# Folding the values of layer 1: one run of matmuls for each pair, two engines to empty its banks, and a bias on VectorE

## Chip, cores and metric

The kernel runs on one core of a Trainium2 chip. The metric is the device time of one execution in microseconds. Every input and output is float32. TensorE multiplies, VectorE (DVE) and ScalarE (ACT) do elementwise work and are the ones that read the matmuls' result banks (PSUM), GpSimd (POOL) does elementwise work, SyncE (SP) issues most transfers.

## What is computed

Two cross-attention layers in sequence, on 4 batches of 1024 tokens with 1024 channels and a context of 64 tokens a batch (the reference, cut; the norm over the context, the masks and the head shapes are left out):

```python
# layer 0: 32 query heads, 8 key heads
out = softmax(q(x) @ k(ctx).T * scale + mask0) @ v(ctx)     # per head
r   = out @ Wo + bo + x
x1  = (r - mean(r)) * rsqrt(var(r) + 1e-6) * gamma + beta
# layer 1: 16 heads
a   = layer_norm(ctx)
out = softmax((x1 @ Wq.T) @ (a @ Wk.T).T * scale) @ (a @ Wv.T)
y   = x1 + tanh(gate) * (out @ Wo.T)
```

## The kernel before

The work is in stages. Stage 1 computes layer 0's queries and attention and leaves its head outputs turned in DRAM (oTd). **Stage 2**, the one that the change is in, multiplies these by Wo, adds bo and x, normalizes, and stores x1. Stage 3 is layer 1.

Layer 1 is folded: since the context has only 64 tokens, keys are multiplied into Wq (`folded_queries`, stage 1) and values into Wo (`folded_values`, in stage 2), once for each batch, so that stage 3 has one 1024x1024 product for the scores and one for the outputs. Both folded matrices go to DRAM (ad and bd) and are read back in stage 3.

**Pairs.** Stage 2 goes over 16 pairs of 128-token tiles (`for pair in range(1, NPAIR)`, L1098; pair 0 is begun before the loop). A pair's product with Wo is Winograd's form of Strassen's algorithm, `products` at L435: seven products of half size, each four matmuls of 128x128x512, with accumulating banks. In the order of the list at L470, called P1 to P7 here:

- P1 = A11 B11 and P2 = S2 T2 and P4 = S1 T1 and P5 = S4 B22 go into one bank X, each added onto what the bank holds; after each, VectorE adds the bank's state to a half row of the result (L455), and the next product of X can only start once that read is done.
- P3 = S3 T3 and P6 = A22 N4 likewise in a bank V; P7 = A12 B21 alone in a bank W.

The sums S1, S2, S4 and S3 of the left side are made by VectorE (`left_out`, L429 to L432) for the next pair, at the place of P6 of the pair before (`tail`). Four banks of 512 columns rotate (pool ps_wx); two tiles of two banks each (pool ps_big, function `two`) serve the fold.

**Rows.** r_0, r_1, ... are tiles of 128 rows x 1024 channels, two for each pair (r_2, r_3 for pair 1). `load_outputs` (L947), called one pair ahead, loads the pair's heads o and its two rows of x into r, and, for all pairs but the first, adds bo to them on GpSimd (L958). The pool of r has six buffers, so a load for pair p + 2 waits until pair p - 1's row has been stored. L455 then adds the products on top. `close_rows` (L1051) normalizes a finished pair on VectorE, a row at a time: two BNStats (L292), an aggregate (L297), L298, a square root on ACT (L299), L306, L302, L309, and a store by SyncE (L1053). These steps are given to the next pair's `project` (L481) as a list `fill`, and a share of it is taken after each of its seven products.

**The fold of the values.** For pair 1 to 8, `folded_values(vT, wch, pair - 1)` is put onto `fill`: one chunk of 128 channels, as two calls of `keys` (one for two batches each). Each call has two pieces (n = 0, 1); a piece is two matmuls, one on the lower and one on the upper 64 rows of TensorE (e = 0, 1), into the two banks of one tile of `two()`. ACT copies both banks, times tanh(gate), to a tile st (L929), and SyncE stores st to bd in two transfers (L933). A chunk thus has four pieces, and two tiles of banks for them. The profile shows each float32 matmul as two records.

The order of instructions on each engine isn't that of the text alone: a scheduler moves them by its own priorities and by the waits between them, except those under `keep_in_program_order`. In the program as built, TensorE's rows of a pair of stage 2 stand as P1, one matmul of P3, P2, the rest of P3, P4, one matmul of P6, P5, the rest of P6, P7, and before the change a chunk of the fold stands behind P7 (in pair 1 in three parts). Each engine works through its own queue in order, and waits at its head.

Of the kernel before, what the change touches and what calls it, by code (L numbers as in the profile page):

```python
# [10 lines left out]
AF = mybir.ActivationFunctionType  # L11
ALU = mybir.AluOpType
# [16 lines left out]
NPAIR = NSUB // 2  # L29
# [42 lines left out]
def tile_two_cross_attentions(  # L72
# [25 lines left out]
    nc = tc.nc  # L98

    def sub_ap(t):  # L100
        return slice(t * P, (t + 1) * P)
# [31 lines left out]
    def open_pool(stack, name, bufs, side="left"):  # L133
        return stack.enter_context(tc.tile_pool(name=name, bufs=bufs, side=side, reuse_waits="tile"))
# [68 lines left out]
    def right_weight(w, tag, name, turned=False):  # L203
        r, loads = right_loads(w, tag, name, turned)
        run(loads)
        return r, right_sums(r)

    def run(steps):
        for s in steps:
            s()  # L210
# [74 lines left out]
    def normalize_steps(t, eps, name, late=False, scaled=None):  # L285

        st = small.tile([P, 2, 6], F32, tag="st", name=f"st_{name}")
        mv = small.tile([P, 2], F32, tag="mv", name=f"mv_{name}")
        rstd = small.tile([P, 1], F32, tag="rstd", name=f"rstd_{name}")

        def stats(i):
            r = nc.vector.bn_stats(st[:, i, :], t[:, i * 512 : (i + 1) * 512])  # L292
            if late:
                tc.keep_in_program_order(r)

        def deviation():
            nc.vector.bn_aggr(mv, st.rearrange("p a b -> p (a b)"))  # L297
            nc.vector.tensor_scalar(rstd, mv[:, 1:2], eps, None, ALU.add)  # L298
            nc.scalar.activation(rstd, rstd, AF.Sqrt)  # L299

        def scale():
            nc.vector.reciprocal(rstd, rstd)  # L302
            if not scaled:
                nc.vector.tensor_scalar(t, t, mv[:, 0:1], rstd, ALU.subtract, ALU.mult)
                return
            nc.vector.scalar_tensor_tensor(t, t, mv[:, 0:1], scaled[0], ALU.subtract, ALU.mult)  # L306

        def shift():
            nc.vector.scalar_tensor_tensor(t, t, rstd, scaled[1], ALU.mult, ALU.add)  # L309

        return [lambda: stats(0), lambda: stats(1), deviation, scale] + ([shift] if scaled else [])
# [73 lines left out]
    tanh_gate = const.tile([P, 1], F32, tag="tanh", name="tanh_gate")  # L385
# [4 lines left out]
    def two():  # L390
        b = big()
        return [b[:, 0:512], b[:, 512:1024]]
# [31 lines left out]
    def left_out(o, pool, name):  # L424

        a11, a21 = o[:, 0:HK, 0:P], o[:, 0:HK, P : 2 * P]
        a12, a22 = o[:, HK:KC, 0:P], o[:, HK:KC, P : 2 * P]
        s = {n: pool.tile([P, HK, P], F32, tag=n, name=f"{n}_{name}") for n in ("S1", "S2", "S4")}
        nc.vector.tensor_tensor(s["S1"], a21, a22, ALU.add)  # L429
        nc.vector.tensor_tensor(s["S2"], s["S1"], a11, ALU.subtract)  # L430
        nc.vector.tensor_tensor(a21, a11, a21, ALU.subtract)
        nc.vector.tensor_tensor(s["S4"], a12, s["S2"], ALU.subtract)  # L432
        return {"A11": a11, "A12": a12, "A22": a22, "S3": a21, **s}
# [443 lines left out]
    def chunk(w, k, name):  # L877
        t = wpool.tile([P, H], F32, tag="wb", name=f"{name}_{k}")
        nc.sync.dma_start(out=t, in_=w[sub_ap(k), :])
        return t  # L880
# [34 lines left out]
    def folded_values(vT, wch, c):  # L915


        def keys(bp):
            st = wpool.tile([P, 2, H], F32, tag="wb", name=f"b_{c}_{bp}")
            for n in range(2):  # L920
                banks = two()
                for e in range(2):
                    q = slice(e * S, (e + 1) * S)
                    nc.tensor.matmul(  # L924
                        banks[e], vT[q, c, sub_ap(bp)], wch[q, n * 512 : (n + 1) * 512],
                        start=True, stop=True,
                    )
                for e in range(2):
                    nc.scalar.activation(  # L929
                        st[:, e, n * 512 : (n + 1) * 512], banks[e], AF.Copy, scale=tanh_gate[:, 0:1]  # L930
                    )
            for b2 in range(2):
                nc.sync.dma_start(  # L933
                    out=bd[bp * 2 + b2, sub_ap(c), :].rearrange("(e s) o -> s e o", e=2),
                    in_=st[b2 * S : (b2 + 1) * S],
                )

        return [lambda bp=bp: keys(bp) for bp in range(2)]

    def load_o(pair, pool, tag="o2"):  # L940
        o = pool.tile([P, KC, 2 * P], F32, tag=tag, name=f"o2_{pair}")
        load = nc.sync.dma_start(out=o, in_=oTd[pair])
        if pair < 2:
            tc.keep_in_program_order(load)
        return o

    def load_outputs(pair):  # L947
        o = load_o(pair, o2pool) if pair > 1 else second if pair else load_o(0, early)
        r = []
        for u in range(2):  # L950
            t = pair * 2 + u
            ru = (rpool.tile([P, H], F32, tag="r", name=f"r_{t}") if pair
                  else early.tile([P, H], F32, tag="r", name=f"r_{t}", bufs=2))
            load = nc.sync.dma_start(out=ru, in_=x[sub_ap(t), :])
            if not pair:
                tc.keep_in_program_order(load)
            if pair:
                nc.gpsimd.tensor_tensor(ru, ru, bo_sb, ALU.add)  # L958
            r.append(ru)
        return o, r  # L960

# [62 lines left out]
    for t in range(last):  # L1024
        n = 28 - AHEAD if t // SUB == NBLK - 2 else 28
        mix(t, (t % SUB + 1) * n // SUB - t % SUB * n // SUB)
    go_on(FOLD_AHEAD)
    n = 4 * KC - FOLD_AHEAD + FIRST
# [22 lines left out]
    def close_rows(pair, r):  # L1051
        def last(u):
            nc.sync.dma_start(out=x1[pair][sub_ap(u), :], in_=r[u])  # L1053

        steps = []
        for u in range(2):
            steps += normalize_steps(
                r[u], EPS0, f"0_{pair * 2 + u}", True, (gamma0_sb, beta0_sb)
            ) + [lambda u=u: last(u)]
        return steps  # L1060
# [3 lines left out]
    def load_x1(pair):  # L1064
        xq = xqpool.tile([P, 2 * NQ, QW], F32, tag="xq", name=f"xq1_{pair}")
        load_quarters(xq, x1[pair])
        return xq

    def turn_x1(pair, xq, pool=None, tag="xT"):

        xT = (pool or xTpool).tile([P, KC, 2 * P], F32, tag=tag, name=f"xT_{pair}")

        def half(h):
            turn_quarters(xq, xT[:, h * HK : (h + 1) * HK, :], (h * HK, (h + 1) * HK))

        def blocks():
            lefts[pair] = left_out(xT, lpool if pool else lxpool, f"x_{pair}")

        return [lambda: half(0), lambda: half(1), blocks]
# [10 lines left out]
    open_stage()  # L1090
    _, ahead_r = load_outputs(1)
    run(first)

    fill = [
        lambda u=u: nc.vector.tensor_tensor(first_rows[u], first_rows[u], bo_sb, ALU.add) for u in range(2)
    ]
    fill += close_rows(0, first_rows)
    for pair in range(1, NPAIR):  # L1098
        r, a = ahead_r, ahead_a
        if pair + 1 < NPAIR:  # L1100
            ahead_o, ahead_r = load_outputs(pair + 1)
        if pair <= KC:
            ahead_w = chunk(wo1, pair, "wo1") if pair < KC else None
            fill += folded_values(vT, wch, pair - 1)
            wch = ahead_w
        if pair == KC + 2:
            w_a, w_a_sums = right_weight(ad[0], "wb", "a0", True)
        if pair in (NPAIR - 3, NPAIR - 2):
            fill += w_a_sums[0:2] if pair == NPAIR - 3 else w_a_sums[2:4]
        if pair == 3:  # L1110
            early_cm.close()
            xTpool = open_pool(last_cm, "x1T", 1)
            lxpool = open_pool(last_cm, "leftx", 1)
            xqpool = open_pool(last_cm, "x1q", 1)
        if pair == NPAIR - 4:
            xq = load_x1(1)
        if pair == NPAIR - 3:
            fill += turn_x1(1, xq)

        def tail():  # L1120
            nonlocal ahead_a
            if pair + 1 < NPAIR:
                ahead_a = left_out(ahead_o, lpool, f"0_{pair + 1}")
            else:
                turned[2]()

        project(a, w_o, r, fill, tail=tail)
        fill = close_rows(pair, r)
        if pair == NPAIR - 2:
            xq = load_x1(0)  # L1130
            turned = turn_x1(0, xq, o2pool, "o2")
            fill = turned[:2] + fill
# [78 lines left out]
    for pair in range(NPAIR):  # L1211
        r = []
        for u in range(2):
            ru = rpool.tile([P, H], F32, tag="r", name=f"r1_{pair}_{u}")
            nc.sync.dma_start(out=ru, in_=x1[pair][sub_ap(u), :])
            r.append(ru)
        fill = []
# [79 lines left out]
```

## Time and profile before

| | |
|---|---|
| median of 3 runs | 1915.06 us (1913.88 to 1915.12) |
| profiled execution | 1915.11 us, span 1913.3 us, granted TensorE clock 0.995 |
| TensorE busy | 1868.9 us (98%) |
| VectorE / ACT / GpSimd busy | 1292.1 (68%) / 427.9 (22%) / 179.1 us (9%) |
| stage 2 | from about 716 to 1130 us |
| L929, ACT's copies of the fold | 64 of 128x512, 687 ns each |
| L958, GpSimd's bias | 30 of 128x1024, 2354 ns each (median) |
| L1095, VectorE's bias for pair 0 | 2 of 128x1024, 1226 ns each |

Times in the profile are in us from the start of the span. A line of the timeline is: start, length, engine, source line, operation, output<-input, count, and in brackets how long the engine had been idle before and whose end released it. SPq, PEq and the like are the engines' sequencers, which issue transfers and wait for semaphores.

### The profile page before, as it was taken

What the parts mean: (1) busy time and instruction counts of PE and PEld (TensorE: products, weight loads), DVE (VectorE), ACT (ScalarE), POOL (GpSimd) and SP (SyncE); (2) the same over time, 40 slices, a digit from 0 to 9 for tenths busy, and PEclk for the clock granted to TensorE, in tenths of its full rate; (3) what the DMA queues carried; (4) which work ended last, traced back from release to release, by engine and by line L of the source; (5) the groups of instructions that cost most, each with busy time, mean ns of one, the idle gap of its engine ahead of it and who ended that gap; (6) DMA issues with size and microseconds to landing.
All of it is one profiled execution on the core that took longest, in us unless ns stands there. A gap on an engine that the chain in (4) does not pass through costs nothing.

```text
span 1913.3 us, 17522 instructions
## 1 busy us (share of the span) xinstructions
PE 1868.9 (98%) x6096; PEld 880.0 (46%) x6096; DVE 1292.1 (68%) x1582; ACT 427.9 (22%) x1396; POOL 179.1 (9%) x212
## 2 busy tenths in 40 slices
PE   8999999999998899999999999999999999999999
PEld 7744444444455653343344444444444444444444
DVE  3425589789878985575568778557665766576653
ACT  1101575666536751212100001000000000000000
POOL 0016011111100103121113100000000000000000
PEclk9999999999999899999999999999999999999999
DMA  8996599899878966567473363466656565657421
GB/s 276 184 222 192 158 253 247 253 252 261 252 186 275 302 234 207 188 207 238 164 218 138 121 141 90 110 165 158 150 143 165 150 158 143 165 142 165 121 88 44
DMA packets 220745, 350.54 MB, mean 183 GB/s; under 512 B 26992, under 2 KB 146160, under 8 KB 215664
## 3 DMA queue, kind: packets, MB, share of 16 engines
q1 hardware_dynamic: 152896, 242.44, 45.8%
q0 software_dynamic: 15216, 60.83, 10.5%
q10 hardware_dynamic: 52544, 46.14, 8.8%
q8 instruction: 48, 0.79, 0.2%
q14 instruction: 41, 0.34, 0.1%
HBM read 207.53 MB, written 141.82 MB: 183 GB/s over the span
## 4 chain that ended last, share of the span: by engine, by line
PE 82%; DVE 8%; DMA 5%; issue 2%; ACT 2%; POOL 0%; SPq 0%; DVEq 0%; POOLq 0%; ACTq 0%
PE wx L446 59%; PE wx L576 14%; PE big L680 2%; DMA pq<-p 2%; PE big L924 1%; PE wx L379 1%; PE big L379 1%; DVE s L684 1%; PE big L759 1%; DMA p<-s 1%; DMA q<-qTd 1%; DVE s L715 1%; DVE mx L691 1%; DVE sm L711 1%; DMA o<-oTd 1%
## 5 line engine op out<-in xcount | busy, mean ns | idle before, releaser
L455 DVE TENSOR_TENSOR r<-wx,r 128x512 f32<-128x512 f32 x224 | 153.5, 686 | 230.1 <-PE wx L446 215.3
L698 ACT ACTIVATE s<-s,mx 128x64 f32<-128x64 f32 x488 | 162.8, 335 | 74.9 <-DVE mx L691 70.7
L502 ACT ACTIVATE s<-s 128x1024 f32<-128x1024 f32 x32 | 33.7, 1057 | 651.7 <-DVE s L501 651.7
L459 DVE TENSOR_TENSOR s<-wx,key_bias 128x512 f32<-128x512 f32 x64 | 44.1, 690 | 136.7 <-PE wx L446 136.7
L446 PE MATMUL wx<-wo_B,S 128*128 128x512 f32 x256 | 117.1, 600 | 1.5 <-DVE r L455 1.5
L576 PE MATMUL wx<-xT,wq_S 128*128 128x512 f32 x256 | 116.5, 598 | 0.8 <-ACT z L587 0.8
L446 PE MATMUL wx<-b_B,pT 128*128 128x512 f32 x256 | 115.8, 593 | 0.6 <-ACT pT L414 0.6
L446 PE MATMUL wx<-b_B,S_p 128*128 128x512 f32 x256 | 116.0, 596 | 0.0
L446 PE MATMUL wx<-a_B,xT 128*128 128x512 f32 x256 | 115.4, 592 | 0.0
L446 PE MATMUL wx<-a_B,S_x 128*128 128x512 f32 x256 | 115.3, 593 | 0.1
L576 PE MATMUL wx<-xB,wq_A 128*128 128x512 f32 x256 | 115.1, 597 | 0.0
L446 PE MATMUL wx<-wo_B,o 128*128 128x512 f32 x256 | 114.8, 596 | 0.0
L958 POOL TENSOR_TENSOR r<-r,bo 128x1024 f32<-128x1024 f32 x30 | 78.5, 2625 | 313.8 <-DMA r<-in_x_dram 159.4
L684 DVE TENSOR_TENSOR s<-big,m 128x1024 f32<-128x1024 f32 x64 | 77.4, 1215 | 28.4 <-PE big L680 26.8
L680 PEld LDWEIGHTS big<-kv,q 64*128 64x128 f32 x1024 | 71.1, 195 | 48.3 <-issue 39.9
L698 ACT ACTIVATION_READ_ACCUMULATOR s<-s,mx 128x1 f32 x488 | 91.4, 187 | 0.0
L680 PE MATMUL big<-kv,q 64*128 64x128 f32 x1024 | 82.6, 292 | 2.6 <-DMA q<-qTd 2.6
L419 DVE STREAM_TRANSPOSE pT<-pq 128x1024 f32<-128x1024 f32 x66 | 78.0, 1219 | 3.3 <-DMA pq<-p 3.3
L446 PEld LDWEIGHTS wx<-wo_B,S 128*128 128x128 f32 x256 | 47.1, 190 | 67.7 <-issue 51.2
L715 DVE TENSOR_TENSOR s<-s,sm 128x1024 f32<-128x1024 f32 x64 | 77.0, 1216 | 0.9
L446 PEld LDWEIGHTS wx<-wo_B,o 128*128 128x128 f32 x256 | 47.8, 190 | 63.5 <-issue 62.3
L446 PEld LDWEIGHTS wx<-a_B,S_x 128*128 128x128 f32 x256 | 48.5, 190 | 62.0 <-issue 58.4
(162 smaller groups left out, 2903.5 us busy)
## 6 DMA issues: line engine op xcount, KB each, us to landing
p<-s POOLq DMA_DIRECT2D x19, 1024.0 KB, 8.1
pq<-p POOLq DMA_DIRECT2D x76, 256.0 KB, 6.0
xq<-in_x_dram SPq DMA_DIRECT2D x64, 256.0 KB, 10.2
q<-qTd SPq DMA_DIRECT2D x32, 512.0 KB, 7.4
oTd<-oT ACTq DMA_DIRECT2D x32, 512.0 KB, 7.4
ad<-a POOLq DMA_DIRECT2D x16, 1024.0 KB, 8.9
o<-oTd SPq DMA_DIRECT2D x16, 1024.0 KB, 5.1
r<-in_x_dram SPq DMA_DIRECT2D x32, 512.0 KB, 5.3
```

What stands on the lines that cost most here:

```text
L379: nc.tensor.matmul(ps[:, 0:256], w[k // HK, c // HK][:, k % HK, sub_ap(c % HK)], ct[:, k, :], start=(k == 0), stop=(k == KC - 1),)
L419: return nc.vector.transpose(dst.rearrange("p k (u i) -> p k u i", i=Q), t[:, :, k0 * Q : k1 * Q].rearrange("p u (k j) -> p k u j", j=Q),)
L446: nc.tensor.matmul(banks[name], a[s][:, k, :], w[m][:, k, :], start=first and k == 0, stop=last and k == HK - 1, skip_group_check=True,)
L455: nc.vector.tensor_tensor(at, bank, at, ALU.add)
L459: nc.vector.tensor_tensor(at, bank.rearrange("p (h s) -> p h s", s=S), bias.unsqueeze(1).to_broadcast([P, 512 // S, S]), ALU.add,)
L502: nc.scalar.activation(s, s, AF.Exp)
L576: nc.tensor.matmul(bank, w_q[a][:, k, sub_ap(i)], rows[b][:, k, :], start=first and k == 0, stop=last and k == HK - 1, skip_group_check=True,)
L680: nc.tensor.matmul(ps[:, at : at + P], q[on, c * 4 + g, :], k0bd[on, b, c, :], start=True, stop=True,)
L684: nc.vector.tensor_tensor(quarters[:, :, c * 8 : (c + 1) * 8], ps.rearrange("p (k a l) -> p a k l", a=NQ, l=Q), mask.rearrange("p e (h l) ...
L698: nc.scalar.activation(heads[:, e, k], heads[:, e, k], AF.Exp, bias=mx[:, e, k : k + 1], accum_out=sm[:, e, k : k + 1],)
L715: nc.vector.tensor_tensor(heads[:, e], heads[:, e], wide(sm[:, e]), ALU.mult)
L958: nc.gpsimd.tensor_tensor(ru, ru, bo_sb, ALU.add)
```

## The change

1. The matmuls of a piece keep their program order relative to other such instructions. Of a piece's two banks, ACT copies the first and VectorE the second (a tensor_scalar with the same factor), each to its own half of st.
2. GpSimd's add of bo in `load_outputs` is gone. Instead `biased(r)` gives two VectorE adds, one for each row. Those of pair 1 are put onto pair 1's `fill` behind the close of pair 0, and those of pair p + 1 onto `fill` in pair p, behind the chunk of the fold.

```diff
@@ folded_values / keys
-                    nc.tensor.matmul(
+                    tc.keep_in_program_order(nc.tensor.matmul(
                         banks[e], vT[q, c, sub_ap(bp)], wch[q, n * 512 : (n + 1) * 512],
                         start=True, stop=True,
-                    )
-                for e in range(2):
-                    nc.scalar.activation(
-                        st[:, e, n * 512 : (n + 1) * 512], banks[e], AF.Copy, scale=tanh_gate[:, 0:1]
-                    )
+                    ))
+
+                nc.scalar.activation(
+                    st[:, 0, n * 512 : (n + 1) * 512], banks[0], AF.Copy, scale=tanh_gate[:, 0:1]
+                )
+                nc.vector.tensor_scalar(
+                    st[:, 1, n * 512 : (n + 1) * 512], banks[1], tanh_gate[:, 0:1], None, ALU.mult
+                )
@@ load_outputs
-            if pair:
-                nc.gpsimd.tensor_tensor(ru, ru, bo_sb, ALU.add)
@@ stage 2
-    fill = [
-        lambda u=u: nc.vector.tensor_tensor(first_rows[u], first_rows[u], bo_sb, ALU.add) for u in range(2)
-    ]
-    fill += close_rows(0, first_rows)
+    def biased(r):
+        return [lambda u=u: nc.vector.tensor_tensor(r[u], r[u], bo_sb, ALU.add) for u in range(2)]
+
+    fill = biased(first_rows) + close_rows(0, first_rows) + biased(ahead_r)
     for pair in range(1, NPAIR):
         r, a = ahead_r, ahead_a
         if pair + 1 < NPAIR:
             ahead_o, ahead_r = load_outputs(pair + 1)
         if pair <= KC:
             ahead_w = chunk(wo1, pair, "wo1") if pair < KC else None
             fill += folded_values(vT, wch, pair - 1)
             wch = ahead_w
+        if pair + 1 < NPAIR:
+            fill += biased(ahead_r)
```

In the changed program as built, a chunk stands behind P5 instead of P7 (in pair 1 with one matmul of P7 between its pieces 2 and 3, in pair 4 with one of P6 between 3 and 4), and VectorE's copy of a piece waits for the semaphore of ACT's copy of that piece.

## The prediction

> **What bounds the kernel now.** I read the page's shares first (PE busy 98% of 1913.3 us), then the busy time of each engine cut at the pairs of stage 2, then the chain of waits through that stage, then the timelines of VectorE, GpSimd and SyncE. Stage 2 runs from 716 to 1130 us; the change touches nothing outside it. Times t below count from the first matmul of a pair's P1.
>
> Cut at the pairs (busy time by engine, then clock and DMA):
>
> ```profile
> core 0: us, PE busy (x) PEld busy (x) DVE busy (x) ACT busy (x) POOL busy (x), PEclk, DMA share, GB/s
> ...
> 780.03:809.45 29.42, 28.89 (x73) 11.71 (x74) 16.38 (x25) 5.22 (x11) 5.66 (x2) 1.00 0.68 215
> 809.45:838.90 29.45, 28.87 (x73) 11.70 (x74) 21.02 (x31) 5.27 (x11) 5.19 (x2) 1.00 0.69 214
> ```
>
> Pairs 2 to 8, each with one chunk of the fold, take 29.35 to 29.45 us whatever VectorE does in them (16 or 21 us). TensorE sets the pace, so only work that makes it wait counts. The chain shows where it waits, in every chunk alike:
>
> ```profile
> 863.49 1.08 PE big L924 x4
> ...
> 864.64 1.27 ACT b L929 x2
> 865.91 0.04 issue
> 865.96 1.13 PE big L924 x4
> 867.09 0.03 issue
> 867.11 1.13 PE big L924 x4
> 868.24 24.67 PE wx L446 x56
> ```
>
> A chunk (four times two matmuls) holds TensorE 4.75 us; its third piece waits for ACT to have emptied both banks of the first, one after the other (1.27 us), and starts 2.47 after the chunk's start, the fourth at 3.62.
>
> The start of stage 2, and one stall late in it (the bracket is idle time and its releaser):
>
> ```profile
> 722.19 6.96 POOL L958 TENSOR_TENSOR r<-r,bo 128x1024 f32<-128x1024 f32 x3 [32.81 <-DVE r L1095]
> 725.31 3.70 PE L446 MATMUL wx<-wo_T,S 128*128 128x512 f32 x8 [0.97 <-DVE r L455]
> 727.85 1.28 SPq L954 DMA_DIRECT2D r<-in_x_dram  x3
> 733.02 8.81 POOL L958 TENSOR_TENSOR r<-r,bo 128x1024 f32<-128x1024 f32 x3 [3.88 <-DMA r<-in_x_dram]
> 1062.94 3.38 DVE L309 SCALAR_TENSOR_TENSOR r<-r,rstd,beta 128x1024 f32<-128x1024 f32 x1
> 1066.98 3.70 PE L446 MATMUL wx<-wo_B,S 128*128 128x512 f32 x8 [0.63 <-DVE r L455]
> ```
>
> At 725.31 TensorE has waited 0.97 for row r_2, whose GpSimd add came first. Rows r_5 to r_7 are issued at 727.85 and the first lands at 733.0. An L309 beside a GpSimd add takes 3.38 us instead of 1.28; three such cases (L309 at 1012.8, 1037.8, 1062.9) cost TensorE 0.44 + 0.43 + 0.63 = 1.5 us.
>
> **The change, part by part.** (1) *ACT and VectorE in turn.* In the changed program, as built, VectorE's copy does not wait for TensorE but for ACT's copy of the same piece: both write one tile, st. So a piece is still emptied in series; but ACT goes on to piece 2 at once. By rows: ACT's copy starts 1.15 after the chunk's start (864.64 - 863.49) and takes 0.69. VectorE's copy is not in the trace; L455 (128x512 from PSUM) takes 0.69, and a bound above comes from L325, a tensor_scalar of 128x256, at 0.535 against 0.425 for the plain copy L323: 0.69 + 0.11 = 0.80. I take 0.75. With 0.05 from semaphore to start, piece 3 starts at 1.15 + 0.69 + 0.05 + 0.75 + 0.05 = 2.69 (before: 2.47), piece 4 when piece 3's matmuls are through, 0.86 later, 3.55 (before: 3.62). Gain 0.07 to 0.1 a chunk if VectorE is punctual. Were the two copies side by side, pieces would start at about 1.9 and 2.75: 0.87 a chunk, the other bound. [...]
>
> (2) *The chunk moves* from after P7 to after P5, so VectorE's order around it changes: L455 of P5, L432 and often a bias add stand ahead of its first copy, and the close of the second row (L292 to L302) now stands between P3's and P4's L455. That chain needs 3.62 us from one L455 to the next place (L309 at 816.73 after L455 at 813.11), and P4's matmuls only 3.43: P5 starts 0.19 later in each of pairs 2 to 8, and in 13 and 14.
>
> (3) *30 bias adds go from GpSimd to VectorE*, at 1.23 us each (L1095, 1226 ns) for 2.35 before. GpSimd is then idle in stage 2: the 1.5 us of stalls and the 0.97 at 725 go. But now each add waits in VectorE's own queue for its row's load, with L455 and the copies behind it.
>
> Pair 1: the order there is L455(P1), add r_4, L455(P2), a BNStats, add r_5, BNStatsAggregate, add r_6, L298, L306, L455(P3), add r_7. TensorE starts P2 0.97 earlier and ends P4 at 733.9; its next matmul (P6) needs L455(P3). VectorE stands at add r_5 until the load lands, 733.0; then 1.23 + 0.2 + 1.23 + 0.15 + 1.2 + 0.7 brings L455(P3)'s end to 737.7: a stall of 3.85. On from there: P6 to 741.2; L455(P4) after add r_7 and L309, end 741.5, P5 to 745.0; chunk at 745.1; its first copy comes after L455, L306, L309 and the adds of r_3 and r_2, at 748.7; piece 3 at 749.5, piece 4 at 750.3, P7 ends 754.05. In the trace pair 2 begins at 750.64. Cost 3.4. Bounds: -0.9 if the loads are no obstacle, +5 if r_6 and r_7 land 1 to 2 us after VectorE gets to them (GpSimd's three adds from 733.02 bound their landing only by their own starts).
>
> Pairs 2 to 8: chunk start T = 18.8; P5's sum can be read at 18.85. VectorE: L455(P4) 14.4, L309, L429, L430, L431 to 18.1, L455(P5) 18.85, L432, free at 20.1; ACT's first copy ends at 18.8 + 1.15 + 0.69 = 20.64. An add ahead of L455(P5) fits where the row has landed by about 18. GpSimd's starts say when it had, at the latest: t = 15.0, 17.5, 18.0, 17.0, 19.0, 16.7, 14.9 for pairs 2 to 8. Pairs 2, 7, 8 (add after L429) and 3 (after L431): hidden. Pair 6 (after L431): add 19.0 to 20.2, copy one at 21.4 instead of 20.7: +0.7. Pair 5 (add right before the first copy): 21.3, +0.6. Pair 4 (add between the first two copies): one P6 matmul fills the gap, two more switches of TensorE between the shapes, about 0.35 in all. The second row's add stands after copy 2 or 3 and waits for a load at t = 25; L455 of P6 and P7 then come at 27.8 and 28.4, before P1's next read at 33: nobody waits. Sum: 7 x (0.19 - 0.08) + 0.7 + 0.6 + 0.35 = 2.4. Bounds: -6.1 (side by side, 7 x 0.87) to +14 (each load 2 us later than now).
>
> Pairs 9 to 15: saved 1.5. The adds of r_24 and r_25 stand after L432 at the end of pair 11, where VectorE is full (back to back from 1015.89 to 1033.88, then L455 of the next P1 at 1034.15): 2 x 1.23 - 0.27 = 2.15 later. The other adds fall into gaps (r_26 and r_27 between L455(P3) at 10.8 and L455(P4) at 14.2). 2 x 0.19 for the pairs 13 and 14. Sum 1.0; bounds -1.5 and +3.5.
>
> SyncE: the four stores at L933 wait for the last copy and come at t = 22 to 31, the loads of o and wo behind them at t = 1 to 9 of the next pair, needed at 16 and 18.8: covered; uncovered, they would hold a chunk for about a landing, 5 us (L954: 5.3).
>
> Sum: 3.4 + 2.4 + 1.0 = 6.8 on the profiled execution's 1915.11 (span 1913.3 and 1.8 around it; the median is 1915.06): **1922 us**. Stages 3 on keep TensorE's pace, so nothing gives it back.
>
> **Rivals.** *A, side by side (faster).* The wait on ACT costs nothing because VectorE would have been later anyway or the copies are short, and rows are there in time: 1915.1 - 6.1 - 1.5 - 0.9 = 1906.6. For it: the chain names ACT at each chunk. Against: the built wait, and VectorE's queue. It decides only if copy one ends by 1.9 after the chunk's start. *B, hidden (no change).* Part (1) as worked out, but in pair 1 the loads land early enough, say by 730: its stall goes, its chunk is punctual and P2's 0.97 stays gained; then -0.9 + 2.4 + 1.0 = +2.5: 1917.6. For it: DMA share there is not full all the time; against: the issue at 727.85 and GpSimd's own wait until 733.02. *C, late rows.* With traffic moved (stores, o, wo behind the chunk), first-row loads land 2 us later in each pair, and copy one with them: 3.4 + 14 + 2 = +19: 1934. For it: 2.6 to 6.7 us between store and load in the trace; against: the stores leave the very time in which row loads run.
>
> **How the numbers follow.** My forecast 0.52 (own range 1918 to 1927), A 0.12, B 0.2, C 0.16. Range: 1912 to 1931, which leaves most of A and the worse half of C outside. About 0.2% (3.8 us: 1911.2 to 1918.9) is what a measurement tells from no change. Faster 0.12; same 0.22 (B and the edge of mine); slower 0.66.
>
> **What would show it.** Pair 1 longer by 3 to 4 us, TensorE idle before L446 with releaser L455 near 734 to 738; VectorE's copies each starting some 0.05 after an ACT copy ends; chunks of 4.6 to 4.8 us in pairs 2, 3, 7, 8 and 5.3 or more in 5 and 6; a wait of some 2 us at the start of pair 12; no VectorE instruction stretched by GpSimd. Wrong: chunks near 3.9 us (A), pair 1 unchanged (B), or VectorE waiting for r's load in every pair with TensorE behind it (C).

## The result, and the profile after

| | before | after |
|---|---|---|
| median | 1913.77 us (1911.84 to 1917.35, 11 runs) | 1918.98 us (1916.58 to 1925.19, 11 runs) |
| ratio, 95% interval | | 1.0026 [1.0019, 1.0034] |
| a second measurement | 1914.3 us (35 runs) | 1918.29 us (8 runs), 1.0022 [1.0011, 1.0033] |
| profiled execution, span | 1915.11, 1913.3 | 1917.05, 1915.0 |
| VectorE / ACT / GpSimd busy | 1292.1 / 427.9 / 179.1 | 1323.5 / 411.1 / 100.6 |

The change makes the kernel 4 to 5 us slower, more than the 0.2% that a measurement tells from no change. In the first measurement its runs lie further apart than before's (8.6 us for 5.5), in the second they don't (4.8 for 10.1), so nothing is read from that.

All of stage 2 can be read from TensorE's timeline: it begins with the first matmul of P7 of pair 0, and ends with the first matmul of stage 3. I cut it at the first matmul of P1 in pair 2 and in pair 9 (where P7 and P1 are one group of records, 3.43 after the group's start). The table has every kernel that ran, each by one trace; the edits follow below.

| kernel | pair 1 | pairs 2-8 | pairs 9-15 | stage 2 | ratio to before [95%] |
|---|---|---|---|---|---|
| before | 34.2 | 205.9 | 173.6 | 413.6 | |
| after | 36.2 | 207.6 | 171.6 | 415.4 | 1.0026 [1.0019, 1.0034] |
| after_again | 38.5 | 207.4 | 171.6 | 417.5 | 1.0022 [1.0011, 1.0033] |
| after_third | 36.0 | 207.6 | 171.6 | 415.2 | one run, 1918.03 |
| order_only | 32.8 | 205.9 | 173.3 | 412.1 | 0.9994 [0.9978, 1.0010] |
| fold_only | 33.6 | 206.8 | 172.7 | 413.1 | 1.0008 [0.9999, 1.0017] |
| bias_only | 39.2 | 212.9 | 171.6 | 423.6 | 1.0044 [1.0030, 1.0058] |
| own_bias | 32.1 | 208.7 | 171.9 | 412.8 | 1.0000 [0.9991, 1.0009] |
| two_tiles | 37.1 | 203.5 | 171.6 | 412.2 | 1.0005 [0.9996, 1.0014] |
| own_two | 32.1 | 208.9 | 171.4 | 412.4 | 0.9996 [0.9985, 1.0006] |
| fold_two | 33.0 | 206.7 | 174.3 | 414.0 | 0.9998 [0.9988, 1.0007] |
| mix | 33.4 | 206.8 | 175.9 | 416.1 | 1.0010 [1.0000, 1.0020] |
| p3pool | 35.7 | 208.7 | 171.6 | 415.9 | 1.0012 [1.0002, 1.0022] |
| best | 33.4 | 200.9 | 172.1 | 406.4 | 0.9967 [0.9954, 0.9979] |

So in the first trace the change lost 2.1 us in pair 1 and 1.7 in the pairs 2 to 8, and won 2.0 in the pairs 9 to 15. Before's share is from one trace. Of the 1.4 by which order_only is shorter in pair 1, 0.28 is a shorter wait before P2 (0.69 for 0.97); the rest goes with the kept order, for in before the chunk's first matmul stands alone there, ahead of P5:

```profile
734.95 1.12 PE L924 MATMUL big<-wo,vT 64*128 64x512 f32 x2
```

The changed kernel's busy time of each engine in the pairs 2 to 5:

```profile
core 0: us, PE busy (x) PEld busy (x) DVE busy (x) ACT busy (x) POOL busy (x), PEclk, DMA share, GB/s
752.44:781.79 29.35, 28.64 (x74) 11.69 (x72) 20.26 (x31) 3.15 (x6) 0.00 (x0) 1.00 0.67 203
781.79:811.11 29.32, 28.55 (x73) 11.73 (x72) 23.15 (x34) 3.15 (x6) 0.00 (x0) 1.00 0.76 225
811.11:842.21 31.10, 29.04 (x73) 11.60 (x72) 22.31 (x35) 3.15 (x6) 0.00 (x0) 1.00 0.66 193
842.21:872.04 29.83, 28.57 (x73) 11.76 (x72) 20.25 (x31) 3.15 (x6) 0.00 (x0) 1.00 0.73 223
```

GpSimd is idle, ACT's time fell from 5.2 to 3.2 a pair, VectorE's rose, and pairs 2 and 3 take 29.35 and 29.32 for 29.39 and 29.42. Pair 4 takes 1.7 more, pair 5 0.4 more. The chain of waits through the chunk of pair 6:

```profile
890.67 1.08 PE big L924 x4
891.75 0.03 ACTq L929
891.78 0.04 issue
891.82 0.70 ACT b L929
892.52 0.02 issue
892.54 0.76 DVE b L932
893.31 0.04 issue
893.35 1.99 PE big L924 x8
```

ACT's copy and then VectorE's run in series: piece 3 starts 2.68 after the chunk's start, and the chunk ends 4.67 after it. The timelines of VectorE and TensorE at the places that lose:

```profile
732.40 1.23 DVE L1095 TENSOR_TENSOR r<-r,bo 128x1024 f32<-128x1024 f32 x1 [3.23 <-DMA r<-in_x_dram]
736.12 0.68 DVE L455 TENSOR_TENSOR r<-wx,r 128x512 f32<-128x512 f32 x1
736.85 3.70 PE L446 MATMUL wx<-wo_N,o 128*128 128x512 f32 x8 [3.00 <-DVE r L455]
747.91 1.99 PE L924 MATMUL big<-wo,vT 64*128 64x512 f32 x8 [0.80 <-DVE b L932]
833.96 1.22 DVE L1095 TENSOR_TENSOR r<-r,bo 128x1024 f32<-128x1024 f32 x1 [1.60 <-DMA r<-in_x_dram]
835.90 1.13 PE L924 MATMUL big<-wo,vT 64*128 64x512 f32 x4 [1.30 <-DVE b L932]
864.02 1.99 PE L924 MATMUL big<-wo,vT 64*128 64x512 f32 x8 [1.26 <-DVE b L932]
```

In pair 1 VectorE stands 3.23 us at the add of a row that isn't loaded yet. L455, which empties P3's bank, is behind it, and TensorE idles 3.00 before P6. In pair 4 an add waits 1.60 for its load with a copy of the fold behind it, and piece 4 is 1.30 late. In pair 5 an add merely stands in front of the first copy: 1.26 of idle time for 0.77 in the other chunks.

### The profile page after: what moved, and what is told of

Read it like the earlier page. It is cut to its first block, busy times and chain, and to the rows that moved or that the text cites. A ratio compares the mean times of both kernels' runs of the same rounds, so it can differ in the third digit from the quotient of the medians.

```text
span 1915.0 us, 17483 instructions
## 1 busy us (share of the span) xinstructions
PE 1865.2 (97%) x6096; PEld 878.2 (46%) x6096; DVE 1323.5 (69%) x1644; ACT 411.1 (21%) x1364; POOL 100.6 (5%) x182
## 4 chain that ended last, share of the span: by engine, by line
PE 81%; DVE 10%; DMA 6%; issue 2%; ACT 1%; POOL 0%; SPq 0%; DVEq 0%; POOLq 0%; ACTq 0%
PE wx L446 58%; PE wx L576 14%; PE big L680 2%; DVE s L684 1%; PE wx L379 1%; PE big L379 1%; PE big L759 1%; PE big L924 1%; DVE s L715 1%; DMA p<-s 1%; DMA q<-qTd 1%; DMA pq<-p 1%; DVE mx L691 1%; DVE sm L711 1%; DMA o<-oTd 1%
## 5 line engine op out<-in xcount | busy, mean ns | idle before, releaser
L455 DVE TENSOR_TENSOR r<-wx,r 128x512 f32<-128x512 f32 x224 | 153.4, 685 | 185.8 <-PE wx L446 185.3
L299 ACT ACTIVATE rstd<-rstd 128x1 f32<-128x1 f32 x32 | 6.5, 203 | 327.3 <-DVE rstd L298 327.3
L446 PEld LDWEIGHTS wx<-a_B,xT 128*128 128x128 f32 x256 | 48.6, 190 | 61.2 <-issue 60.3
```

The lines of the kernel that those rows point to most:

```text
L446: nc.tensor.matmul(banks[name], a[s][:, k, :], w[m][:, k, :], start=first and k == 0, stop=last and k == HK - 1, skip_group_check=True,)
L455: nc.vector.tensor_tensor(at, bank, at, ALU.add)
```

## The experiments

**Undoing the place of the adds (own_bias).**

```diff
-    fill = biased(first_rows) + close_rows(0, first_rows) + biased(ahead_r)
+    fill = biased(first_rows) + close_rows(0, first_rows)
@@ in the loop, behind the chunk
-        if pair + 1 < NPAIR:
-            fill += biased(ahead_r)
+        fill += biased(r)
```

> The whole change, but a pair's rows get bo in their own pair, behind its chunk on the list, not a pair ahead: the loads have landed long before. As built, one add stands behind L432 directly ahead of the chunk's first copy. My theory: no VectorE instruction waits for a load of r in pairs 1 to 8, pair 1's stall of 3 us is gone or below 1, piece 3 starts 0.5 to 0.7 later than in the change (3.2 to 3.4 after the chunk's start) in each chunk, sum 1915 to 1918, and the times of the runs scatter less than the change's 8.6 us. Rival (the time follows the place of the chunk and VectorE's load, not the waits for loads): 1919 to 1922, and the scatter stays.

Measured: 1914.93 us, ratio 1.0000 [0.9991, 1.0009], runs from 1910.5 to 1915.9. No add waits for a load in the pairs 1 to 8, and pair 1 has no stall. An add does stand in front of the first copy, in each chunk:

```profile
769.64 1.22 DVE L1095 TENSOR_TENSOR r<-r,bo 128x1024 f32<-128x1024 f32 x1
770.78 1.40 DVE L932 TENSOR_SCALAR b<-big,tanh_gate 128x512 f32<-128x512 f32 x2
771.58 1.99 PE L924 MATMUL big<-wo,vT 64*128 64x512 f32 x8 [1.26 <-DVE b L932]
```

Everything else of the change is still there, so its loss comes from adds that are queued on VectorE a pair ahead, before their rows have landed. By the table what comes back is pair 1's (32.1 for 36.2): in the pairs 2 to 8 the adds in front of the first copies cost more than the waits in the pairs 4 and 5 did (208.7 for 207.6).

**Each half alone (fold_only, bias_only, order_only).** fold_only is before with the first hunk of the change alone, so its adds are GpSimd's; bias_only takes back that hunk and keeps the rest; order_only is before plus the kept order of a piece's matmuls.

```diff
@@ bias_only: after, with
-                    tc.keep_in_program_order(nc.tensor.matmul(
+                    nc.tensor.matmul(
...
+                for e in range(2):
+                    nc.scalar.activation(
+                        st[:, e, n * 512 : (n + 1) * 512], banks[e], AF.Copy, scale=tanh_gate[:, 0:1]
+                    )
@@ order_only: before, with
-                    nc.tensor.matmul(
+                    tc.keep_in_program_order(nc.tensor.matmul(
```

> Only the fold's part of the change; the adds of bo stay on GpSimd, and the chunk stays behind P7. My theory (the loss lies in VectorE's queue, which holds for the loads of rows): 0 to -1 us against before, ratio 0.999 to 1.001, about 1913 to 1915; piece 3 starts about 2.7 after the chunk's start where VectorE is punctual, pair 1 as before with its 0.97 before P2, GpSimd's stretched VectorE instructions still there. Rival (emptying the banks in turn by two engines is what costs): 4 to 5 us slower than before, as the whole change.

> Only the bias's part: the adds on VectorE, ACT copies both banks as before and the matmuls of a piece keep no order. As built the chunk stands around P5 and its first two matmuls are torn apart by P5. My theory: at least as slow as the whole change, +5 to +13 against before (pair 1's stall of about 3, adds that wait for loads, and up to 1 us per chunk for torn pieces). Rival (the fold costs, the bias is harmless): ratio 0.999 to 1.001.

> Of the whole change only the kept order of a piece's matmuls; ACT empties both banks, GpSimd adds bo. Both theories: as before, ratio 0.999 to 1.001; the chunk behind P7 in every pair, 4.75 long.

fold_only: 1.0008 [0.9999, 1.0017], 1916.67 us at a before of 1913.99. Its interval leaves room for a loss of up to 0.17%, so the fold is not shown to be free. Its trace is of the fastest of its runs (1912.31); it has 0.5 less than before in stage 2, and 1.4 more in pair 4 (cut behind P1, since a part of the chunk slid into the next P1), where TensorE waited 1.68 for VectorE's copy. I hadn't expected that; fold_two shows it better. order_only: 0.9994 [0.9978, 1.0010], no difference. bias_only: 1923.62 us, 1.0044 [1.0030, 1.0058], worse than the whole change, as my theory had it: pair 1 has its stall (3.52), and each chunk is torn:

```profile
770.76 1.12 PE L924 MATMUL big<-wo,vT 64*128 64x512 f32 x2
771.82 3.70 PE L446 MATMUL wx<-wo_B,S 128*128 128x512 f32 x8
775.45 1.98 PE L924 MATMUL big<-wo,vT 64*128 64x512 f32 x6
```

One matmul of the first piece stands alone in front of P5, its partner behind. One matmul alone (two records) holds TensorE for 1.06, as long as two side by side (the four records of 1.08 in the chain above). A pair of stage 2 takes 30.1 to 30.7 instead of 29.4. bias_only lacks the second engine as well as the kept order; but a lone matmul's 1.06 is seen directly. So in the whole change the kept order does useful work: it keeps a piece's two matmuls, which use different halves of TensorE's rows, side by side.

**The wait between the two copies (two_tiles, own_two).** The prediction said that VectorE's copy waits for ACT's because both write one tile, st. two_tiles leaves st as it is and makes two PSUM tiles of the two banks; in its trace VectorE's copies no longer wait for ACT. So the tie is the two-bank tile of `two()`.

```diff
-        b = big()
-        return [b[:, 0:512], b[:, 512:1024]]
+        return [ps_big.tile([P, 512], F32, tag="half", name="half") for _ in range(2)]
```

(ps_big is closed ahead of stage 2's loop, opened with four one-bank tiles, and opened as before ahead of stage 3. Source lines move by one or two. own_two has own_bias's edit too.)

> The whole change, but with a piece's two banks as two tiles of PSUM, so that VectorE's copy waits for TensorE alone. My theory: piece 3 starts about 2.0 after the chunk's start and a chunk takes 3.9 to 4.1 where no add is late (pairs 2, 3, 7, 8), 4 to 5 us in all below the change, about 1914 to 1915; pair 1's stall and pair 4's stay. Rival (VectorE's queue is late at each chunk anyway, so the wait on ACT costs nothing): 1918 to 1919.5 as the change.

> Two tiles for a piece, and the adds of bo on VectorE in the rows' own pair, so that one stands directly ahead of VectorE's first copy in each chunk. My theory (VectorE must be free when the first piece is through, or two tiles bring nothing): the copy ends at the same 3.2 after the chunk's start as with one tile, a chunk is still 5 us or more, and the time is within 1.5 us of the form with one tile, 1913 to 1916. Rival (ACT's half coming free early is worth its part): 1909 to 1911.

two_tiles: 1914.70 us, 1.0005 [0.9996, 1.0014], 4.1 us less in the pairs 2 to 8, pair 1 unchanged (stall 3.21). My theory held for the sum; a chunk took 4.35 in pair 2 and not 3.9 to 4.1, since VectorE comes to its copy late. The timeline of the two copies:

```profile
771.52 4.35 PE L924 MATMUL half<-wo,vT 64*128 64x512 f32 x16
772.68 0.69 ACT L929 ACTIVATE b<-half,tanh_gate 128x512 f32<-128x512 f32 x1 [6.46 <-PE half L924]
773.08 1.41 DVE L932 TENSOR_SCALAR b<-half,tanh_gate 128x512 f32<-128x512 f32 x2
773.54 0.69 ACT L929 ACTIVATE b<-half,tanh_gate 128x512 f32<-128x512 f32 x1 [0.17 <-PE half L924]
```

ACT and VectorE read different banks at the same time (773.54 to 774.23), ACT at its usual 0.69, VectorE at 0.70 a copy, as for two in a row elsewhere. own_two: 1913.96 us, 0.9996 [0.9985, 1.0006], 0.4 less than own_bias in stage 2: with an add ahead of the copy two tiles bring next to nothing, as expected.

**The fold's gain without the adds (fold_two, mix).** fold_two is two_tiles with the second part of the change taken back, so that GpSimd adds bo. In mix GpSimd adds it for the pairs 2 to 9, and VectorE for pair 1 in the rows' own pair and for the pairs 10 to 15 a pair ahead; mix is two_tiles with

```diff
+            if 2 <= pair <= 9:
+                nc.gpsimd.tensor_tensor(ru, ru, bo_sb, ALU.add)
@@
-    fill = biased(first_rows) + close_rows(0, first_rows) + biased(ahead_r)
+    fill = biased(first_rows) + close_rows(0, first_rows)
@@ in the loop, behind the chunk
-        if pair + 1 < NPAIR:
+        if pair == 1:
+            fill += biased(r)
+        if 10 <= pair + 1 < NPAIR:
             fill += biased(ahead_r)
```

> The fold's part alone with a piece's two banks as two tiles; the adds of bo stay on GpSimd and the chunk behind P7. My theory (in a chunk only the third piece's wait costs; the loss of the whole change came from the adds): each chunk falls from 4.75 to 3.9 to 4.1, seven times 0.65 to 0.85, and 0.5 in pair 1, so stage 2 is 5 to 6.5 us shorter than before and the time about 1908 to 1909. Rival (TensorE is held by VectorE's copy all the same, as in the two-tile form of the whole change, whose pairs 2 to 8 saved 2.3): 1911 to 1912.

> Two tiles for a piece, as before; bo is added by GpSimd for the pairs 2 to 9, by VectorE for pair 1 (in its own pair) and for the pairs 10 to 15 (a pair ahead). My theory: the gains add up, pair 1 shorter by 0.7 to 2 than before, seven chunks by 0.65 to 0.85, pairs 9 to 15 by 1.95 as in every form without GpSimd's adds: -7 to -9 us against before, 1905 to 1907. Rival (gains in pairs 9 to 15 depend on the fold's place or on all the adds being gone): 1908 to 1910, as the fold's part with two tiles.

Both missed by 6 to 10 us: 1914.58, 0.9998 [0.9988, 1.0007], and 1915.92, 1.0010 [1.0000, 1.0020]. The chunks are as expected (3.92, and TensorE doesn't wait in them; 28.59 to 28.61 a pair in six of seven, cut behind P1), but pair 4 of fold_two takes 35.2. Its timeline, and the busy time of the engines in steps of 2 us (columns as in the view by pairs; the granted clock stands behind the five engines):

```profile
829.60 2.36 DVE L419 STREAM_TRANSPOSE xT<-xq 128x1024 f32<-128x1024 f32 x2
833.77 0.74 DVE L932 TENSOR_SCALAR b<-half,tanh_gate 128x512 f32<-128x512 f32 x1
834.57 1.13 PE L924 MATMUL half<-wo,vT 64*128 64x512 f32 x4 [1.39 <-DVE b L932]
836.43 2.07 PE L924 MATMUL half<-wo,vT 64*128 64x512 f32 x2 [0.73 <-DVE b L932]
838.43 5.91 PE L446 MATMUL wx<-wo_B,o 128*128 128x512 f32 x8
```

```profile
832.00:834.00 2.00, 1.18 (x4) 0.29 (x2) 1.97 (x4) 1.38 (x3) 0.00 (x0) 1.00 0.92 340
834.00:836.00 2.00, 1.13 (x4) 0.30 (x4) 2.00 (x4) 0.23 (x1) 0.00 (x0) 1.00 0.89 361
836.00:838.00 2.00, 1.57 (x2) 0.50 (x2) 1.04 (x2) 0.46 (x1) 1.18 (x1) 0.52 0.17 41
838.00:840.00 2.00, 2.00 (x3) 0.84 (x3) 0.75 (x1) 0.00 (x0) 1.16 (x1) 0.50 0.96 197
840.00:842.00 2.00, 2.00 (x3) 0.67 (x2) 0.00 (x0) 0.00 (x0) 0.00 (x0) 0.50 1.02 258
```

In pair 4 VectorE has stage 3's two transposes and sums ahead of its first copy, which comes 3.6 after the chunk's start. TensorE idles 1.39 and 0.73, and then its granted clock falls to 0.50 for 6.8 us (836.09 to 842.91): a product that takes 3.70 takes 5.91. The stalls are 2.1 of the 6.6 lost, 6.8 us at half speed about 3.4. In mix the same happens in pair 4, and a stall with half clock behind it again in pair 12:

```profile
1035.30 2.35 DVE L1099 TENSOR_TENSOR r<-r,bo 128x1024 f32<-128x1024 f32 x2
1035.40 1.02 PE L446 MATMUL wx<-wo_T,o 128*128 128x512 f32 x2
1038.31 5.40 PE L446 MATMUL wx<-wo_T,S 128*128 128x512 f32 x8 [1.89 <-DVE r L455]
```

These are the adds of r_24 and r_25, directly ahead of L455(P1). And in pair 9, where mix goes over to adds a pair ahead, the first one waits for its load as in pair 1 of the change, with a copy and L455 behind it, and TensorE stalls 1.22 at 963.28:

```profile
960.74 1.23 DVE L1099 TENSOR_TENSOR r<-r,bo 128x1024 f32<-128x1024 f32 x1 [3.23 <-DMA r<-in_x_dram]
```

**Two more traces of the changed kernel (after_again, after_third).** No edit.

> The changed kernel again, for a second trace. My theory (what the change loses is waits for the loads of rows in VectorE's queue, and these differ from execution to execution): pair 1's stall before P6 between 2 and 5 us, and the waits of the adds in pairs 3 to 8 at other places or of other size than in the first trace, the chunks where no add waits at 4.67 as before. Rival (the waits are fixed by the order): the same stalls within 0.2 us in the same pairs.

> The changed kernel a third time, one trace. Theory: the stall before P6 in pair 1 follows the landing of the row loads and lies between 2.5 and 4.5; where it is longer than about 3.4, the granted clock falls to 0.5 for some 3 us behind it and the eight records of P6 take 5 or more instead of 3.70; where it is shorter, neither. The rest of stage 2 within 0.5 us of the first two traces. Rival (clock and stall have nothing to do with each other): a dip without a long stall, or a long stall without a dip.

The stalls of the pairs 4 to 8 are the same in all three traces within 0.2: there the rival was right, they are fixed by the order. Pair 1's stall varies: 3.00, 3.68 and 2.81. Behind the longest one the clock fell, and P6 took 5.40:

```profile
735.35 5.40 PE L446 MATMUL wx<-wo_N,o 128*128 128x512 f32 x8 [3.68 <-DVE r L455]
```

```profile
732.33:735.74 3.41, 0.40 (x1) 0.30 (x2) 3.41 (x6) 0.20 (x1) 0.00 (x0) 1.00 0.05 22
735.74:739.16 3.42, 3.42 (x5) 1.35 (x4) 3.42 (x5) 0.00 (x0) 0.00 (x0) 0.50 0.18 75
739.16:742.57 3.41, 3.41 (x9) 1.53 (x8) 2.10 (x4) 0.00 (x0) 0.00 (x0) 1.00 0.19 78
```

That trace lost 4.3 in pair 1, the other two about 2. So stage 2 is 1.6, 1.8 and 3.9 longer than before's, while the medians differ by 4 to 5. What is left shows in the granted clock of the whole run, as a mean over the runs: 0.9941 and 0.9942 after, 0.9951 to 0.9956 before; 0.0012 of 1915 us is 2.3. The other two forms with adds a pair ahead in pair 1 have 0.9943 and 0.9944 (two_tiles, bias_only), and own_bias, own_two and order_only, without that stall, 0.9953 to 0.9955. That the clock falls behind pair 1's stall in most executions would fit, but one of three traces shows it, and best and fold_only have 0.9947 and 0.9945 without that stall; this part stays open.

**Pair 1 alone (p3pool).**

```diff
+            if 1 <= pair <= 3:
+                nc.gpsimd.tensor_tensor(ru, ru, bo_sb, ALU.add)
@@
-    fill = biased(first_rows) + close_rows(0, first_rows) + biased(ahead_r)
+    fill = biased(first_rows) + close_rows(0, first_rows)
@@
-        if pair + 1 < NPAIR:
+        if 4 <= pair + 1 < NPAIR:
```

> The whole change, but GpSimd adds bo for the rows of the pairs 1 to 3 as before, so that VectorE has no add to wait at in pair 1; from pair 4 on the adds are VectorE's, a pair ahead, as changed. My theory (pair 1 is most of the loss: its stall of 3 to 3.7 costs 2, and where it is longer than about 3.3 TensorE's clock falls to half after it, which costs another 2 to 3 in most executions): no stall before P6 in pair 1, no dip of the granted clock in stage 2, 3.5 to 5 us below the change, 1913.5 to 1915.5. Rival (the adds that wait in pairs 4 and 5 and the place of the chunk are the loss): 1917 to 1919.

1917.05 us, 1.0012 [1.0002, 1.0022], on the rival's side of my bounds, while its ratio lies half way between the change and before. It doesn't separate the two: the stall before P6 is gone, but GpSimd's adds cost pair 1 two stalls of their own, 1.84 and

```profile
732.73 3.48 DVE L309 SCALAR_TENSOR_TENSOR r<-r,rstd,beta 128x1024 f32<-128x1024 f32 x1
737.46 3.70 PE L446 MATMUL wx<-wo_B,S 128*128 128x512 f32 x8 [1.59 <-DVE r L455]
```

an L309 stretched from 1.28 to 3.48 beside a GpSimd add, with L455 behind it. In pair 3, where TensorE also waits 0.54 before P2, and in pair 6, matmuls of P6 stand between pieces 3 and 4 of the chunk. How much of the loss is pair 1's is therefore known only from the traces (2 to 4 us, and 4.1 between the change and own_bias).

**A faster version (best).** mix, with the adds of the pairs 10 to 15 in the rows' own pair, and ACT for both banks in pair 4:

```diff
+                if c == 3:
+                    nc.scalar.activation(
+                        st[:, 1, n * 512 : (n + 1) * 512], banks[1], AF.Copy, scale=tanh_gate[:, 0:1]
+                    )
+                else:
                     nc.vector.tensor_scalar(
...
-        if pair == 1:
+        if pair == 1 or pair >= 10:
             fill += biased(r)
-        if 10 <= pair + 1 < NPAIR:
-            fill += biased(ahead_r)
```

> Two tiles for a piece; bo added by GpSimd for the pairs 2 to 9 and by VectorE, in the rows' own pair, for pair 1 and the pairs 10 to 15; in pair 4, where VectorE is full (two transposes and stage 3's sums), ACT empties both banks. My theory (two tiles gained 0.82 in each of six chunks, and lost it in pair 4, where the late VectorE copy idled TensorE and its clock fell to half for 6 us): no dip of the clock in stage 2, pair 4 within 0.5 of 29.4, pairs 9 to 15 shorter by about 2: 6 to 8 us below before, 1906 to 1908.5. Rival (a TensorE without idle time loses clock elsewhere, so that the gain is given back): 1911 to 1915 with a mean granted clock below 0.994.

1908.41 us for 1915.19, ratio 0.9967 [0.9954, 0.9979]: faster than both kernels, within the expectation. Stage 2 is 7.2 shorter than before: 0.7 in pair 1, 5.0 in the pairs 2 to 8, 1.5 in the pairs 9 to 15; the granted clock is 1.00 in all of it, and the longest stall is 1.03, at the end of pair 11. Its chunks of pair 2 and 4:

```profile
775.03 3.99 PE L924 MATMUL half<-wo,vT 64*128 64x512 f32 x16
832.23 4.76 PE L924 MATMUL half<-wo,vT 64*128 64x512 f32 x16
```

## Why the prediction came out as it did

The direction and the first mechanism were right: adds in VectorE's own queue wait for loads with L455 and the copies behind them, and TensorE waits for those. By the forecast's terms, against the first trace:

- *Part (1), the fold.* Piece 3 at 2.69: 2.68. VectorE's copy 0.75: 0.739 to 0.751. Chunk shorter by 0.08: 4.67 for 4.75. Only the cause of the series was wrong: not st, but the one PSUM tile of two banks. The other bound (0.87 a chunk, side by side) was nearly reached by fold_two, 0.83.
- *Part (2), the moved chunk.* The 0.19 by which the close chain should delay P5 did not show: in pair 2 P5 starts 4.42 after P4 for 4.38 before, and a plain pair takes 29.33, 0.1 less than before.
- *Pair 1, +3.4:* mechanism and place right, size too high in two traces (2.1 and 1.9) and too low in one (4.3). The stall was 3.00 for 3.85, as the row was there 0.4 sooner than by the trace of before, and instructions of VectorE overlap a little more than I allowed: from the first add to L455's end 4.4 for 4.7. What the forecast didn't have is the clock: a longer stall can cost more than its own length.
- *Pairs 2 to 8, +2.4:* 1.7, but with the terms in other places. Pair 4 cost 1.7 instead of 0.35, a term that no run shows by itself: the add between the copies was taken as punctual, but waits 1.60 for its load. Pair 5 0.4 for 0.6. Pair 6 nothing for 0.7: its row was there in time.
- *Pairs 9 to 15, +1.0:* this step failed; they won 2.0. The 2.15 for the adds of r_24 and r_25 came to 0.17 + 0.25. They do stand ahead of L455(P1), but in the changed program three matmuls of P3, not one, lie between P1 and P2 in pair 12 and cover them. In mix, with one, the same adds cost 1.89: price right, cover overlooked. The 1.5 of stalls did go; with the 0.42 that makes -1.1, and the other 0.9 of the gain was in no term of the forecast.

The sum of the trace is thus +1.8 where I had +6.8; the median rose by 5.2. The forecast of 1922 lies 3.0 above the median, and that closeness is in good part luck: terms that were 5.0 too high on the trace, 3.0 of it in the pairs 9 to 15, stood in for a loss of some 3 that the trace does not show.

Rival A (side by side) failed as the wait was built; two_tiles gained 4.1 over the change in the pairs 2 to 8, which is 2.4 over before, where A had 6.1. Rival B (pair 1 without a stall) failed on the load, which landed at 732.4 and not by 730. Rival C (rows later in every pair) failed: plain pairs take 29.33.

## What to carry to other kernels

An instruction that waits for a transfer belongs on an engine whose queue holds nothing urgent, or behind the point where the transfer has surely landed; put a pair ahead into the queue of the engine that frees TensorE's banks, it hands its wait on (in pair 1 VectorE waited 3.23 us for the load, and TensorE 3.00 for VectorE). Two engines emptied a piece's banks at the same time here only where the banks are separate tiles (a chunk of 4.67 us with one tile, 3.92 with two), and that gained little where the second engine wasn't free at that moment (own_two is 0.4 shorter than own_bias in stage 2, two_tiles 3.2 shorter than the change); check the fullest pass of the loop (pair 4 here), not the typical one. A stall of TensorE can cost more than its length: behind some of those of 1.39 to 3.68 us the granted clock was 0.50 for 3.4 to 6.8 us, behind others of 1.84 to 3.21 it stayed at 1.00.

## What the hardware did that I had not expected

- *Half clock behind stalls.* The granted clock stayed at 1.00 behind stalls before P6 of 2.81 (after_third), 3.00 (the first trace of the change) and 3.21 (two_tiles), and fell to 0.50 behind 3.52 (bias_only, for 6.8 us; P6 took 6.47) and 3.68 (after_again, for 3.4 us; P6 took 5.40). It also fell behind 1.89 in mix (for 3.4 us), and behind 1.39 and 0.73 close together in fold_two (for 6.8 us), but not behind 1.84 in p3pool. The length alone thus doesn't decide; what else does, these runs leave open. The 3.3 and 3.4 in the expectations of p3pool and after_third are estimates that lie between the 3.21 and the 3.52; with 1.89 in mix they are no bound for other places. The first trace at its stall of 3.00 (733.85 to 736.85):

```profile
734.00:736.00 2.00, 0.00 (x0) 0.00 (x0) 2.00 (x3) 0.20 (x1) 0.00 (x0) 1.00 0.06 23
736.00:738.00 2.00, 1.15 (x3) 0.67 (x4) 2.00 (x5) 0.00 (x0) 0.00 (x0) 1.00 0.00 0
```

- *VectorE beside GpSimd.* A GpSimd add of 128x1024 again and again stretched a VectorE instruction by some 2 us (3.48 for 1.28 in p3pool). Every form without such adds in the pairs 9 to 15, and without a long stall there, takes 171.4 to 172.1 for them; before and the forms with the adds take 172.7 to 174.3.
